# The first sequence's norm, queries and keys of a last attention given out inside the dense layer ahead of it, and maxima that run 30 steps ahead instead of 36

## The chip, the core and the metric

The kernel runs on one core of a Trainium2 chip, in one launch. A core has a matrix engine (TensorE, PE in the profile; its weight loads are counted apart as PEld), three engines for elementwise work (VectorE, DVE; ScalarE, ACT, with the activation functions; GpSimd, POOL), and SyncE (SP), which here issues nearly all transfers. Every engine runs its own list of instructions in order and waits on semaphores for what the others make. The metric is the device time of a launch in microseconds (us); the time of a kernel is the median of its runs.

## The reference

Four sequences of 1024 tokens with 128 features go through two blocks, eight residual layers in all: gated linear attention, mixture of experts, causal softmax attention, the same mixture of experts, then a rotary linear attention, a dense layer, a softmax attention with a linear distance bias ("the last attention"), and the dense layer once more. Ahead of each stands a layer norm without weights. The two layers around the change:

```python
# last attention, on x = _layernorm(x): 16 heads of 8 features
q, k, v = jnp.split(x @ W_attn + b_attn, 3, axis=-1)      # each (4, 1024, 16, 8)
att = jnp.einsum('bqhd,bkhd->bhqk', q, k) * (1.0 / math.sqrt(D))
att = att / temperature
bias = slopes[:, None, None] * rel[None, :, :]            # rel = key position - query position
bias = jnp.where(causal[None, :, :], bias, -jnp.inf)
w = jax.nn.softmax(att + bias[None, :, :, :], axis=-1)
y = jnp.einsum('bhqk,bkhd->bqhd', w, v).reshape(Bc, Tc, Cc)
return y @ W_proj + b_proj
...
# dense layer, on x = _layernorm(x): 128 -> 512 -> 512 -> 512 -> 128, weights of -1, 0, 1 with scales
h = silu(_tlin(x, w1_w, w1_s)) * _tlin(x, w2_w, w2_s)
h = gelu(_tlin(h, h1_w, h1_s)); h = gelu(_tlin(h, h2_w, h2_s))
return _tlin(h, w3_w, w3_s)
```

The causal attention has the same form with 16 heads of 8 query and key features, 64 value features and no bias.

## The kernel before, in words

**Stages.** The activations `k.x` stay on the core throughout. The stages run one behind another, each with its own pools; what of the next layer can be done early is mixed into the layer ahead by hand. A scheduler then orders the instructions of each engine, so that the order in the code is a priority, not the final order.

**Two softmax attentions, one loop.** `softmax_attention` serves the causal ("ca") and the last ("aa") attention. Two heads make a pair; 4 sequences have 32 pairs, and a round of the main loop takes two of them. A round has 24 steps: 12 tiles of (half of the queries, block of 128 keys) for each of its two pairs. A step makes a tile of scores on PE (`product`, L721, and the mask through `hide`, L727), then its exponential on ACT (L849); the products with the values follow (L968 in ca, L1138 in aa).

**Maxima ahead.** The exponential needs each query's largest score. The generator `maxima` computes it apart, with the scores the other way round: 12 steps for a pair (`BY_QUERY`), in each two matmuls (L721, out to `bank`) and two reductions on DVE (L749 with the causal mask, L754 without). When a pair's 12 steps are done, `finish` transposes the result (L763), splits it into a high and a low part (L765 on ACT, L767 on DVE) and writes them with four transfers (L771, SP) into two rows of the pair's query operand; the scores multiply these rows along, and so subtract the maximum. `all_maxima` strings the pairs together; `finish` of a pair comes behind the first step of the next. Ahead of the first round, 36 steps are called (three pairs); after that one step goes with each step of the main loop, until all are used up.

**Operands.** `Pairs` holds six query and six key tiles in turn (`held`). A `prologue(b)` makes a sequence's queries and keys: layer norm (`k.normed`, L104 to L125), transposes (L90), projections (L1100, evacuated with bias on DVE in L1103 and L1105), a split into high and low part (L1106 on ACT, L1107 on POOL), and `lay_out`, eight transfers in all to two images in DRAM, where heads lie in rows (L701). `load(n)` reads a pair's operands back in four transfers (L710). The last attention's prologue also computes the values (L1115, L1119) into a tile that `clear` sets up on POOL (L1089, L1090). Sequence 0's prologue and the loads of four pairs come ahead of the maxima, sequence b+1's in round 4b + 1. Ahead of all of it `alibi_attention` computes the scale from the temperature (L1078, L1079) and multiplies two biases (L1082, L1083).

**The dense layer.** `dense_layer` branches on a flag in memory; the side that runs here takes each product in two parts, high and low. `dense_parts` works in eight lots of 512 tokens with five stages each; 22 ticks with two lanes run two lots side by side, a lane two ticks behind the other. Its lines: input transposes L1383, splits L1390 to L1394, products L1400, the gate L1421 and L1423, the Gelus L1440 to L1446, the output L1453, its transposes L1457 and the residual sum L1460. In the first dense layer a generator `ahead` runs beside: 16 pieces ahead of the ticks, then one with every lane of every tick. It holds the rotary attention, `Rotary.pieces`, 10 pieces for each sequence. Its tables and weights lie in a pool `ra_w` that `third.close()` gives back behind the layer.

Of the kernel before, what the change touches and what calls it, by code (L numbers as in the profile page):

```python
# [25 lines left out]
DK = P // H  # L26
# [9 lines left out]
class Core:  # L36
# [3 lines left out]
    def __init__(self, ctx: ExitStack, tc: tile.TileContext):  # L40
        self.tc, self.nc = tc, tc.nc
        nc = tc.nc
        self.const = ctx.enter_context(tc.tile_pool(name="const", bufs=1))
        self.x = self.const.tile([P, NT, P], F32, name="x")
        self.ident = self.const.tile([P, P], F32, name="ident")
        make_identity(nc, self.ident)
        self.ones = self.const.tile([P, P], F32, name="ones")
        nc.gpsimd.memset(self.ones, 1.0)
        self.turn = 0
        self.mark = []  # L50
# [730 lines left out]
BY_QUERY = [(i, c) for i in range(NB) for c in range(i // 4 + 1)]  # L781
# [1 line left out]


def softmax_attention(
    k: Core, pairs: Pairs, work, ps_e, scale, maxima, prologue, consume, hold, beside, before=lambda b: None
):

    nc = k.nc
    per = H // 2
    count = B * per

    def all_maxima():
        finish = None
# [12 lines left out]
    def some(n=1):  # L812
        for _ in range(min(n, len(later))):
            later.popleft()()

    turn = 0

    prologue(0)
    for n in range(4):
        pairs.load(n)  # L820
    for _ in range(len(BY_QUERY) * 3):
        next(ahead, None)
    late = None
    for first in range(0, count, 2):
        if first % per == 0 and first // per + 1 < B:
            before(first // per + 1)
        if first % per == 2 and first // per + 1 < B:
            prologue(first // per + 1)
        for n in (first + 4, first + 5):
            if n < count:  # L830
                pairs.load(n)
        for c, j in BY_KEY:
            start = max(j * P, c * 512)
            w = (c + 1) * 512 - start
            es = []
# [215 lines left out]
class AlibiWeights:  # L1051
    def __init__(self, k: Core, pool, wq_d, wk_d, wv_d, bq_d, bk_d, bv_d, wo_d, bo_d, temp_d):
        self.wq = k.load(pool, "aa_wq", wq_d)
        self.wk = k.load(pool, "aa_wk", wk_d)
        self.wv = k.load(pool, "aa_wv", wv_d)
        self.bq = k.load(pool, "aa_bq", bq_d)
        self.bk = k.load(pool, "aa_bk", bk_d)
        self.bv = k.load(pool, "aa_bv", bv_d)
        self.wo = k.load(pool, "aa_wo", wo_d)
        self.bo = k.load(pool, "aa_bo", bo_d)  # L1060
        self.scale = k.load(pool, "aa_scale", temp_d.partition_broadcast(P))


def alibi_attention(k: Core, pairs: Pairs, weights: AlibiWeights):

    nc, tc = k.nc, k.tc
    space = bass.MemoryType.PSUM
    with (
# [4 lines left out]
        tc.tile_pool(name="aa_pse", bufs=2, space=space) as ps_e,  # L1073
        tc.tile_pool(name="aa_pso", bufs=1, space=space) as ps_o,
    ):
        wq, wk, wv, wo = weights.wq, weights.wk, weights.wv, weights.wo
        bq, bk, bv, bo, scale = weights.bq, weights.bk, weights.bv, weights.bo, weights.scale
        nc.vector.reciprocal(scale, scale)  # L1078
        nc.vector.tensor_scalar_mul(scale, scale, 1.0 / math.sqrt(DK))  # L1079

        ps = k.bank()
        nc.tensor.matmul(ps[:1, :P], lhsT=bv, rhs=wo, start=True, stop=True)  # L1082
# [7 lines left out]
            nc.gpsimd.memset(v[:, :, :, DK : DK + 1], 1.0)  # L1090

        def prologue(b):
            xnT = k.normed(two, b, 1)
            for which, (w, bias) in enumerate(((wq, bq), (wk, bk))):
                hi = two.tile([P, T], F32R, tag="hi", name="hi", bufs=1)
                lo = two.tile([P, T], F32R, tag="lo", name="lo", bufs=1)
                for c in range(2):
                    cut = slice(c * 512, (c + 1) * 512)
                    ps = k.bank()
                    nc.tensor.matmul(ps, lhsT=w, rhs=xnT[:, cut], start=True, stop=True)  # L1100
                    val = two.tile([P, 512], F32, tag="val", name="val")
                    if which == 0:
                        nc.vector.tensor_scalar(val, ps, bias, scale, ALU.add, ALU.mult)  # L1103
                    else:
                        nc.vector.tensor_scalar(val, ps, bias, None, ALU.add)  # L1105
                    nc.scalar.copy(hi[:, cut], val)  # L1106
                    nc.gpsimd.tensor_sub(lo[:, cut], val, hi[:, cut].bitcast(F32))  # L1107
                pairs.lay_out(b, which, hi, lo)
            v = vs[b % 2]
            if b < 2:  # L1110
                clear(v)
            for t in range(0, NB, 4):
                ps = k.bank()
                for i in range(4):
                    nc.tensor.matmul(  # L1115
                        ps[:, i * P : (i + 1) * P], lhsT=xnT[:, (t + i) * P : (t + i + 1) * P], rhs=wv,
                        start=True, stop=True,
                    )
                nc.scalar.copy(  # L1119
                    v[:, t : t + 4, :, :DK], ps.rearrange("p (t h d) -> p t h d", t=4, d=DK)  # L1120
                )

        held = {}

        def consume(b, r, c, j, es):
# [55 lines left out]

        softmax_attention(
            k, pairs, work, ps_e, 1.0, partial(pairs.maxima, pool=two, steps=BY_QUERY), prologue, consume,
            False, deque(),
        )


# [154 lines left out]
        }  # L1342


def dense_layer(k: Core, f: Dense, name, before=None, out_d=None):

    flag = k.nc.values_load(f.inexact[0:1, 0:1], min_val=0, max_val=1)
    with k.tc.If(flag == 0) as whole:  # L1350
        dense_parts(k, f, name, True, before, out_d)
    with whole.Else():
        dense_parts(k, f, name, False, before, out_d)


def dense_parts(k: Core, f: Dense, name, exact, before, out_d):

    nc, tc = k.nc, k.tc
    nc_h = NH // P
# [3 lines left out]
    with tc.tile_pool(name=f"ff_{name}{n_parts}", bufs=2) as pool, tc.tile_pool(name=f"ff_{name}{n_parts}w", bufs=1) as wp:  # L1363
        w = f.short if exact else f.load(k, wp)
# [105 lines left out]
        def all_before():  # L1470
            for b in range(B):
                yield from before(pool, b)

        ahead = all_before() if before else iter(())
        for _ in range(16):
# [3 lines left out]
        for tick in range(5 * B + 2):  # L1479
            for lane in range(2):  # L1480
                n, stage = divmod(tick - 2 * lane, 5)
                if 0 <= n < B:
                    next(lots[2 * n + lane])
                next(ahead, None)


@with_exitstack
def kernel(ctx: ExitStack, tc: tile.TileContext, a: dict, out: bass.AP):
    k = Core(ctx, tc)
    dram = ctx.enter_context(tc.tile_pool(name="dram", bufs=1, space=bass.MemoryType.DRAM))  # L1490
    wp = ctx.enter_context(tc.tile_pool(name="moe_w", bufs=1))
    if True:
# [46 lines left out]
        pairs = Pairs(k, rows, images, "aa", 6, NEAR)  # L1539
        aa = []  # L1540
        ff_w = ctx.enter_context(tc.tile_pool(name="ff_w", bufs=1, side="right"))
        third = ExitStack()
        ra_w = third.enter_context(tc.tile_pool(name="ra_w", bufs=1, side="right"))
        rotary = []

        def next_layers():
# [18 lines left out]
            rotary[0].bring = bring  # L1565
        moe.close()
        with k.psum("third", 4, 2):
            dense_layer(k, f, "0", rotary[0].pieces)
        third.close()
        alibi_attention(k, pairs, aa[0])  # L1570
        with k.psum("fourth", 4, 2):
            dense_layer(k, f, "1", None, out)


_DENSE = ["ff_w1", "ff_w2", "ff_h1", "ff_h2", "ff_w3"]
# [132 lines left out]
```

## Time and profile before

| | us |
|---|---|
| three runs | 2610.53, 2607.05, 2591.27; median 2607.05 |
| profiled execution | 2596.9 |
| its span, from first to last instruction | 2595.2 |
| PE busy | 2277.0 (88% of the span) |
| PE weight loads | 1252.7 (48%) |
| DVE busy | 1654.5 (64%) |
| ACT busy | 1244.3 (48%) |
| POOL busy | 916.9 (35%) |
| causal attention, first to last exponential's round | 360.8 to 1299.8 |
| first dense layer, its last transposes | 1666.5 |
| last attention, first exponential | 1735.5 |
| last attention, end of the last round | 2371.8 |
| mean granted PE clock | 0.914 |

The profiled execution is one run of its own, so its length differs from the three timed ones. "Busy" is time in which an engine had an instruction running; matmuls are pipelined, so that a busy PE isn't PE at its peak. Times inside the program are counted from the start of the span. A tile is named by what writes it and what it reads: `bank<-aa_k,aa_q` is a matmul of the maxima in the last attention, `scores<-aa_q,aa_k` one of its scores.

### The profile page before, as it was taken

Reading aid. Unit: us, or ns where it says so; the run is one execution under the profiler, and the core shown is the slowest. Engines: PE = TensorE matmul, PEld = TensorE weight load, DVE = VectorE, ACT = ScalarE, POOL = GpSimd, SP = SyncE. Lnnn points to the kernel's source line nnn. Section 1 sums busy time; section 2 is a strip of 40 time slices with the busy share of each in tenths; the row PEclk is TensorE's granted clock in tenths of the full one; section 3 lists DMA queues with packets and bytes.
Section 4 is the critical chain, followed back from the end, with each engine's and each line's share of the span. In section 5 each row is a group of like instructions: output and inputs, shape, how many; then the busy total and the mean of one; then the engine's idle time right before and its main releaser. Section 6 shows DMA issues by size and latency. Waiting matters only on the chain.

```text
span 2595.2 us, 40054 instructions
## 1 busy us (share of the span) xinstructions
PE 2277.0 (88%) x14195; PEld 1252.7 (48%) x14195; DVE 1654.5 (64%) x4765; ACT 1244.3 (48%) x2023; POOL 916.9 (35%) x718
## 2 busy tenths in 40 slices
PE   6885679998899889988967999769999999998988
PEld 4564533443444344343353666535445454544666
DVE  6977266667667757774146665567767767673544
ACT  6552214545445535454422566405545555455865
POOL 2213306787487567768733332300000000000222
PEclk8977859999899989999988999858989999998999
DMA  9300322001201110000050000042103131010000
GB/s 251 108 9 29 102 73 74 26 18 42 73 25 37 58 50 18 18 22 22 1 167 9 9 25 1 5 126 86 46 23 109 32 98 47 23 23 1 9 9 18
DMA packets 92390, 124.81 MB, mean 48 GB/s; under 512 B 13210, under 2 KB 66460, under 8 KB 92172
## 3 DMA queue, kind: packets, MB, share of 16 engines
q1 hardware_dynamic: 88860, 115.76, 15.8%
q0 software_dynamic: 2560, 5.30, 0.6%
q8 instruction: 120, 1.97, 0.3%
q10 hardware_dynamic: 752, 0.98, 0.1%
q14 instruction: 98, 0.80, 0.1%
HBM read 67.57 MB, written 52.85 MB: 46 GB/s over the span
## 4 chain that ended last, share of the span: by engine, by line
PE 54%; DVE 19%; issue 10%; POOL 8%; ACT 5%; DMA 4%; SPq 0%; DVEq 0%; POOLq 0%; ACTq 0%
PE bank L721 9%; PE o L1138 8%; PE o L968 7%; PE scores L721 7%; PE bank L1400 6%; POOL e_first L986 4%; DVE nm L754 3%; DVE junk L749 3%; PE scores L727 2%; PE bank L932 2%; DVE s L250 2%; PE bank L917 1%; POOL slots L505 1%; PE bank L90 1%; DMA back<-answer,given 1%
## 5 line engine op out<-in xcount | busy, mean ns | idle before, releaser
L849 ACT ACTIVATE e<-scores 128x1024 f32<-128x1024 f32 (+3 forms) x704 | 544.5, 791 | 604.6 <-PE scores L727 370.4
L986 POOL TENSOR_TENSOR e_first<-e_first,e 128x1024 f32<-128x1024 f32 (+3 forms) x320 | 542.2, 1723 | 317.2 <-ACT e L849 178.0
L749 DVE CUSTOM_DVE_ANT_0 junk<-bank,mask 128x128 f32<-128x128 f32 (+3 forms) x1024 | 495.4, 484 | 226.8 <-PE bank L721 162.8
L754 DVE TENSOR_REDUCE nm<-bank 128x1 f32<-128x512 f32 x512 | 332.0, 685 | 126.4 <-PE bank L721 117.1
L968 PE MATMUL o<-e,v 128*32 128x512 f32 (+3 forms) x2560 | 299.9, 494 | 0.0
L721 PE MATMUL bank<-aa_k,aa_q 62*128 62x512 f32 (+3 forms) x768 | 238.8, 434 | 44.1 <-DVE nm L754 25.3
L1138 PE MATMUL o<-e,v 128*32 128x512 f32 (+3 forms) x1536 | 227.5, 517 | 0.0
L721 PE MATMUL bank<-ca_k,ca_q 62*128 62x512 f32 (+3 forms) x768 | 195.5, 422 | 31.2 <-DMA ca_k<-ca_k 14.0
L721 PE MATMUL scores<-ca_q,ca_k 64*128 64x512 f32 (+3 forms) x768 | 182.2, 444 | 36.1 <-ACT e L849 32.3
L721 PEld LDWEIGHTS scores<-ca_q,ca_k 64*128 64x128 f32 x768 | 78.3, 188 | 260.2 <-ACT e L849 185.3
L727 PE MATMUL scores<-halves 64*128 64x128 f32 x2048 | 199.8, 260 | 0.0
L727 PEld LDWEIGHTS scores<-halves 64*128 64x128 f32 x2048 | 193.1, 194 | 10.1 <-issue 0.3
L1107 POOL TENSOR_TENSOR lo<-val,hi 128x512 fp32r<-128x512 f32 x16 | 20.1, 1274 | 442.1 <-ACT hi L1106 260.1
L721 PEld LDWEIGHTS bank<-aa_k,aa_q 62*128 62x128 f32 x768 | 121.4, 203 | 109.0 <-DVE nm L754 53.0
L721 PE MATMUL scores<-aa_q,aa_k 64*128 64x512 f32 (+3 forms) x768 | 164.9, 415 | 2.2 <-ACT e L849 2.0
L1446 DVE TENSOR_TENSOR h<-val,h 128x512 fp32r<-128x512 f32 x128 | 90.9, 717 | 107.8 <-ACT h L1445 78.0
L1006 DVE RECIPROCAL raw<-raw 128x128 f32<-128x128 f32 x128 | 117.5, 937 | 55.1 <-ACT raw L1002 42.7
L1400 PE MATMUL bank<-h,ff_h1s 128*128 128x512 f32 x512 | 135.4, 408 | 15.4 <-POOL h L1394 10.4
L1390 POOL CAST h<-gate 128x512 fp32r<-128x512 f32 x32 | 27.5, 861 | 335.5 <-DVE gate L1423 326.9
L721 PEld LDWEIGHTS scores<-aa_q,aa_k 64*128 64x128 f32 x768 | 80.1, 193 | 135.4 <-issue 67.5
L721 PEld LDWEIGHTS bank<-ca_k,ca_q 62*128 62x128 f32 x768 | 97.5, 201 | 89.8 <-DVE nm L749 36.5
L1440 ACT ACTIVATE val<-bank,ff_t 128x512 f32<-128x512 f32 x128 | 88.1, 689 | 93.3 <-PE bank L1400 84.6
(276 smaller groups left out, 3724.6 us busy)
## 6 DMA issues: line engine op xcount, KB each, us to landing
aa_q<-aa_q SPq DMA_DIRECT2D x64, 208.0 KB
ca_q<-ca_q SPq DMA_DIRECT2D x64, 128.0 KB
ca_k<-ca_k SPq DMA_DIRECT2D x64, 128.0 KB
aa_k<-aa_k SPq DMA_DIRECT2D x64, 128.0 KB
wi<-in_moe_wi_dram SPq DMA_DIRECT2D x16, 256.0 KB
wo<-in_moe_wo_dram SPq DMA_DIRECT2D x16, 256.0 KB
back<-blank SPq DMA_DIRECT2D x8, 512.0 KB
got<-back SPq DMA_DIRECT2D x8, 512.0 KB
```

The costliest lines, as they stand in the source:

```text
L721: self.k.nc.tensor.matmul(out, lhsT=lhsT, rhs=rhs, start=True, stop=stop, skip_group_check=True)
L727: self.k.nc.tensor.matmul(ps, lhsT=part[:, 0, :], rhs=part[:, 1, :], start=False, stop=(a == 1), skip_group_check=True,)
L749: nc.vector.tensor_tensor_reduce(junk[:, :cols], ps[:, :cols], self.mask[:, 512 - cols :], -1.0, 3e38, ALU.add, ALU.min, to,)
L754: nc.vector.tensor_reduce(to, ps[:, :cols], AX.X, ALU.max, negate=True)
L849: power = nc.scalar.activation(e[:, :, :w], ps[:, :, :w], AF.Exp, scale=scale)
L968: nc.tensor.matmul(outs[which][32 * i : 32 * i + 32, skip:], lhsT=v[:, j, i, 32 * which : 32 * which + 32], rhs=es[i // 2][:, i % 2, : 512 ...
L986: nc.gpsimd.tensor_add(to, to, es[i][:, :, : 512 - skip])
L1006: nc.vector.reciprocal(part, part)
L1138: nc.tensor.matmul(o[32 * i : 32 * i + 32, skip:], lhsT=v[:, j, 4 * r + i, :], rhs=es[i // 2][:, i % 2, : 512 - skip], start=(j == 0), sto ...
L1400: nc.tensor.matmul(ps, lhsT=weights[:, c, :], rhs=inputs[c][i], start=(s == 0), stop=(s == len(steps) - 1))
L1440: nc.scalar.activation(val, ps, AF.Gelu, scale=s[:, o : o + 1])
L1446: nc.vector.tensor_sub(nxt[1][:, o, :], val, hi.bitcast(F32))
```

## The change

Five edits:

- The body of the last attention's prologue becomes a generator `alibi_front`, without the values; it norms in two halves of four blocks. Sequences 1 to 3 call it from `prologue` in one go, and `values` behind it.
- For sequence 0 it is run as `alibi_ahead`, which `dense_layer` takes as `then` and appends to the pieces beside the first dense layer, behind the rotary's 40. It has five pieces (the norm, the transposes, the queries, the keys, the loads of four pairs), in ticks 12 to 14 of 0 to 21. Whatever is left is run behind the ticks.
- There it borrows tiles: `Other` maps the tags `xn`, `hi`, `lo` and `val` to the rotary's `ra_xn`, `ra_qT`, `ra_v` and `ra_other`, one buffer each, and the transposed input goes into the rotary's cosine table. `ra_w` therefore stays open to the end of the kernel.
- `softmax_attention` gets `begun`: the last attention no longer calls `prologue(0)` and the first loads.
- Ahead of the first round, both attentions call 30 steps of maxima instead of 36.

```diff
 def softmax_attention(
-    k: Core, pairs: Pairs, work, ps_e, scale, maxima, prologue, consume, hold, beside, before=lambda b: None
+    k: Core, pairs: Pairs, work, ps_e, scale, maxima, prologue, consume, hold, beside, before=lambda b: None,
+    begun=False,
 ):
...
-    prologue(0)
-    for n in range(4):
-        pairs.load(n)
-    for _ in range(len(BY_QUERY) * 3):
+    if not begun:
+        prologue(0)
+        for n in range(4):
+            pairs.load(n)
+
+    for _ in range(len(BY_QUERY) * 2 + 6):
         next(ahead, None)
...
+def alibi_front(k: Core, pairs: Pairs, weights: AlibiWeights, pool, b, to=None):
+    nc = k.nc
+    xn = pool.tile([P, NB, P], F32, tag="xn", name="xn", bufs=1)
+    for i in range(0, NB, 4):
+        k.layernorm(pool, xn[:, i : i + 4, :], k.x[:, b * NB + i : b * NB + i + 4, :], 4)
+    yield
+    weights.xnT = xnT = to or pool.tile([P, T], F32, tag="xnT", name="xnT", bufs=1)
+    k.transpose(xnT, [xn[:, t, :] for t in range(NB)])
+    yield
+    for which, (w, bias) in enumerate(((weights.wq, weights.bq), (weights.wk, weights.bk))):
+        hi = pool.tile([P, T], F32R, tag="hi", name="hi", bufs=1)
+        lo = pool.tile([P, T], F32R, tag="lo", name="lo", bufs=1)
+        for c in range(2):
...
+            val = pool.tile([P, 512], F32, tag="val", name="val", bufs=2)
...
+        pairs.lay_out(b, which, hi, lo)
+        yield
+
+def alibi_ahead(k: Core, pairs: Pairs, weights: AlibiWeights, pool, table):
+    tags = {
+        "xn": ("ra_xn", 1), "hi": ("ra_qT", 1), "lo": ("ra_v", 1), "val": ("ra_other", 1),
+    }
+    pool = Other(pool, tags)
+    weights.invert(k)
+    yield from alibi_front(k, pairs, weights, pool, 0, table)
+    for n in range(4):
+        pairs.load(n)
...
         def prologue(b):
-            xnT = k.normed(two, b, 1)
...
+            for _ in alibi_front(k, pairs, weights, two, b):
+                pass
+            values(b, weights.xnT)
+
+        def values(b, xnT):
             v = vs[b % 2]
...
+        values(0, weights.xnT)
...
-            False, deque(),
+            False, deque(), begun=True,
...
         def all_before():
             for b in range(B):
                 yield from before(pool, b)
+            if then:
+                yield from then(pool)
...
+        for _ in ahead:
+            pass
...
-        third = ExitStack()
-        ra_w = third.enter_context(tc.tile_pool(name="ra_w", bufs=1, side="right"))
+        ra_w = ctx.enter_context(tc.tile_pool(name="ra_w", bufs=1, side="right"))
...
-            dense_layer(k, f, "0", rotary[0].pieces)
-        third.close()
+            dense_layer(
+                k, f, "0", rotary[0].pieces, lambda pool: alibi_ahead(k, pairs, aa[0], pool, rotary[0].cosT)
+            )
```

More of the change, by code (lines that the diff above doesn't have):

```diff
@@ L1060, in __init__, with invert, tile @@
         self.bo = k.load(pool, "aa_bo", bo_d)
-        self.scale = k.load(pool, "aa_scale", temp_d.partition_broadcast(P))
+        self.temp = k.load(pool, "aa_temp", temp_d.partition_broadcast(P))
+        self.scale = pool.tile([P, 1], F32, name="aa_scale")
+    def invert(self, k: Core):
+        k.nc.vector.reciprocal(self.scale, self.temp)
+        k.nc.vector.tensor_scalar_mul(self.scale, self.scale, 1.0 / math.sqrt(DK))
+class Other:
+    def __init__(self, pool, tags):
+        self.pool, self.tags = pool, tags
+    def tile(self, shape, dtype, tag, name, bufs=None):
+        tag, number = self.tags.get(tag, (tag, bufs))
+        return self.pool.tile(shape, dtype, tag=tag, name=name, bufs=number)
@@ new lines, in alibi_front @@
+def alibi_front(k: Core, pairs: Pairs, weights: AlibiWeights, pool, b, to=None):
[11 more added lines that the diff above has]
+        for c in range(2):
+            cut = slice(c * 512, (c + 1) * 512)
+            ps = k.bank()
+            nc.tensor.matmul(ps, lhsT=w, rhs=xnT[:, cut], start=True, stop=True)
+            val = pool.tile([P, 512], F32, tag="val", name="val", bufs=2)
+            if which == 0:
+                nc.vector.tensor_scalar(val, ps, bias, weights.scale, ALU.add, ALU.mult)
+            else:
+                nc.vector.tensor_scalar(val, ps, bias, None, ALU.add)
+            nc.scalar.copy(hi[:, cut], val)
+            nc.gpsimd.tensor_sub(lo[:, cut], val, hi[:, cut].bitcast(F32))
+        pairs.lay_out(b, which, hi, lo)
+        yield
@@ L1075, in alibi_attention @@
     ):
[L1076 to L1079, printed above, removed]
+        wv, wo, bv, bo = weights.wv, weights.wo, weights.bv, weights.bo
         ps = k.bank()
@@ L1092, in prologue @@
         def prologue(b):
-            xnT = k.normed(two, b, 1)
[L1094 to L1108, printed above, removed]
+            for _ in alibi_front(k, pairs, weights, two, b):
+                pass
+            values(b, weights.xnT)
+        def values(b, xnT):
             v = vs[b % 2]
@@ L1342, in load, with dense_layer, dense_parts @@
         }
-def dense_layer(k: Core, f: Dense, name, before=None, out_d=None):
+def dense_layer(k: Core, f: Dense, name, before=None, then=None, out_d=None):
     flag = k.nc.values_load(f.inexact[0:1, 0:1], min_val=0, max_val=1)
     with k.tc.If(flag == 0) as whole:
-        dense_parts(k, f, name, True, before, out_d)
+        dense_parts(k, f, name, True, before, then, out_d)
     with whole.Else():
-        dense_parts(k, f, name, False, before, out_d)
-def dense_parts(k: Core, f: Dense, name, exact, before, out_d):
+        dense_parts(k, f, name, False, before, then, out_d)
+def dense_parts(k: Core, f: Dense, name, exact, before, then, out_d):
     nc, tc = k.nc, k.tc
@@ L1567 @@
         with k.psum("third", 4, 2):
-            dense_layer(k, f, "0", rotary[0].pieces)
-        third.close()
+            dense_layer(
+                k, f, "0", rotary[0].pieces, lambda pool: alibi_ahead(k, pairs, aa[0], pool, rotary[0].cosT)
+            )
         alibi_attention(k, pairs, aa[0])
         with k.psum("fourth", 4, 2):
-            dense_layer(k, f, "1", None, out)
+            dense_layer(k, f, "1", out_d=out)
 _DENSE = ["ff_w1", "ff_w2", "ff_h1", "ff_h2", "ff_w3"]
```

## The prediction

> **What bounds the kernel now.** I read the page's slices first. TensorE (PE) works 88% of the span; its dip in the 26th and 27th of 40 slices (64.9 us each, so 1622 to 1752; 7 and 6 tenths) lies where the first dense layer hands over to the last attention, and the granted clock dips with it (8 and 5):
>
> ```profile
> PE   6885679998899889988967999769999999998988
> PEclk8977859999899989999988999858989999998999
> ```
>
> Then the chain of waits from 1590 to 1900 us (start, length, what). The dense layer's last matmuls (L1457) end at 1666.8; norm, queries, keys and a run of transfers follow, rows to memory and back as operands, until the first matmul of the maxima (L721):
>
> ```profile
> 1666.91 2.83 issue
> 1670.60 1.48 issue
> 1678.28 2.29 PE bank L90 x8
> ...
> 1687.42 6.03 DMA aa_q<-lo
> 1693.61 2.49 POOL lo L1107 x2
> 1696.67 5.50 DMA aa_k<-lo
> 1702.25 2.24 DMA aa_k<-aa_k
> 1704.62 3.24 PE bank L721 x7
> ```
>
> So 1704.6 - 1666.8 = 37.8 us pass, most of it on DMA and POOL. Third, the windows: busy time of PE, PE's weight loads, VectorE (DVE), ScalarE (ACT), POOL, then clock.
>
> ```profile
> 1680.00:1690.00 10.00, 6.73 (x27) 3.88 (x25) 9.94 (x36) 2.76 (x6) 2.55 (x2) 0.84 0.42 136
> 1690.00:1700.00 10.00, 0.00 (x0) 0.00 (x0) 2.87 (x22) 1.34 (x3) 2.48 (x2) 0.50 0.83 256
> 1710.00:1720.00 10.00, 8.47 (x17) 4.46 (x16) 8.59 (x26) 0.00 (x0) 0.00 (x0) 0.50 0.32 80
> 1760.00:1770.00 10.00, 10.00 (x47) 5.10 (x46) 5.15 (x17) 2.39 (x6) 0.00 (x0) 0.50 0.00 0
> ```
>
> DVE is full from 1680 to 1690: it takes the norm statistics of all four sequences in the gap (32 of L104 start from 1670.3 to 1691.3), not just the first. After the gap, maxima run at half clock with PE and DVE both near 85%, and full clock returns at 1770. Last, how quickly a row of maxima is ready (transpose L763, then its last row write on SP):
>
> ```profile
> 1855.33 0.28 PE L763 MATMUL bank<-ident,least 128*16 128x128 f32 x1
> 1858.35 0.62 SPq L771 DMA_DIRECT2D aa_q<-nm_lo  x1
> ```
>
> **The change, part by part.** Times are against the profiled execution, 2596.9 us (span 2595.2 and 1.7 around it); the three runs' median, 2607.05, lies 10.2 above it.
>
> *The front leaves the gap.* In the built program the first sequence's projections, eight row writes and the reads of four pairs stand well ahead of the dense layer's branch end. The layer has 22 ticks with two pieces each; of the 40 rotary pieces 16 go ahead of them, so the rotary ends in the 12th tick and the front takes the next three. The lot that ends in the 15th tick has its last transposes (L1457) at 1606.3, the layer's last at 1666.5: 60 us lie behind the front, and transfers of 6.0, 5.5 and 2.2 us end there unseen. On SP they pass only rotary's four fetches, issued before. PE needs after the branch only the bias product and the eight value matmuls (0.27 each, L1115, at most twice that at half clock): ready for maxima by 1670.4 + 4 = 1674.5.
>
> But DVE is not. In the built order 16 L104 (0.26), 8 L105 (0.16), two chains of small operations (L107, L110, L113 to L116, some 0.85 each), the bias sum (0.24) and one L125 (0.34) stand ahead of the first maximum. From 1672.1 (the exit and a 1.5 us issue gap stay) that is 4.2 + 1.3 + 1.7 + 0.6 = 7.8, so about 1679.5. The first L749 was at 1705.1: **-25.6**.
>
> *Norms of the other sequences lose their cover.* Behind that, among the maxima, stand another 7 L125 (2.4), 8 L105 (1.3), 8 L104 (2.1) and two chains (2.0): 7.8 us in a stretch where DVE has some 15% free. Between 0 (the half-clock PE hides them) and 7.8, I take half: **+4**. ACT gets two Sqrt in mid-attention, with four table loads of 1.28 (none there before); at 0 to 2 us busy of 10 there I put them at +1, bound 0 to 5.1.
>
> *30 steps for 36, last attention.* Twelve steps are a pair's: L763 of the first two pairs lie at 1720.6 and 1735.8, 15.2 us, so 1.27 a step. Six fewer: **-7.5**. They run at the end instead: the two-pair rounds, by the starts of their exponentials (L849), take 35.7 us with 24 steps of maxima, 30.6 with 12, 26.8 with none, so 0.4 a step, **+2.4**.
>
> *The same, causal attention.* L763 at 347.3 and 361.5 give 1.18 a step, **-7**. At the end, rounds 14 and 15 take 55.2 and 52.1 although with 12 and no steps; full rounds take 48.5 to 49.1. In round 14 PE waits 2.35 us for POOL's L1012, behind a queue of L986. Six steps of PE work put in just there cost between +3 (at 0.5 each) and -5 (the round falls toward 49): I take **-1**.
>
> *The dense layer grows.* PE: 8 transposes (1.09 at 1793.2) and four projections (1.98 + 1.88): 5. ACT: 0.6 + 4 x 0.62 + 2 x 0.21 + two to four table loads of 1.28 = 6 to 9. DVE: 8 x (0.26 + 0.16 + 0.34) + two chains + 0.7 + 4 x 0.75 = 11.5. POOL: 4 x 1.25 = 5. PE is 92% busy there (18.09 and 18.76 of 20 us from 1620), so its 5 count nearly in full; the rest is half hidden, but the stand-in tiles have one buffer: a second `val` waits for POOL's subtraction on DVE, with the dense layer's h splits queued behind it, and key `hi` waits on ACT for the query writes' landing (6.0) with Gelus behind. From +5 to +14; **+8**, near the PE price.
>
> Extra layer norm calls in halves, `invert` moved and the rotary weights kept to the end cost nothing: the first lies in the DVE rows counted, the others change no waiting instruction.
>
> Sum: -25.6 + 4 + 1 - 7.5 + 2.4 - 7 - 1 + 8 = **-25.7**, about -26, so 2571 on the profiled execution and 2581 on the median of the runs. I predict between: **2576**. What is late next is DVE, then the half clock, which both stay.
>
> [...] The row: from 1710 to 1770 PE was 85 to 100% busy and was granted 0.50 throughout but for some 4 us near 1745; full clock came at 1681.8, after 3.5 us without a gap, and at 1770, again after four. [...]
>
> **Rivals.**
>
> *Full clock early.* With operands ready, values and maxima stream without a gap and the clock returns some 30 us sooner. PE is the limit at half clock from 1738 to 1770 (windows 8.9 to 10 of 10), worth 15 us: 2561. For it: 1681.8. Against: DVE-paced maxima have gaps. [...]
>
> *Cover gone.* All 7.8 of the norms on the path, tables 5, dense +14, causal tail +3: -25.6 + 7.8 + 5 - 7.5 + 2.4 - 7 + 3 + 14 = -8, 2589 to 2599, so 2594. For it: DVE is in order, and the maxima behind it pace PE. Against: PE at half clock has the same load.
>
> *Not ready in time (slower).* Row writes of a pair are needed by the scores at the next round's start. Thirty steps leave five steps between, not eleven. By rows of the steady round, the fifth-last product (1864.5) lies 7.7 us before that score (1872.2). L763 to the end of the last issue is 1858.97 - 1855.33 = 3.6, with landing (nearest row 2.24) 5.9. If SP holds the eight operand reads of the next pairs (1869.41 to 1872.70, 3.3 us) ahead of them and POOL or ACT adds 0.9, PE waits 10.1 - 7.7 = 2.4 us a round. Over 30 rounds that is +72: 2576 + 72 = 2648. It decides from 0.9 us a round, where it eats the 26. For it besides: nine of the 64 pairs took 10.1 to 16.0 us from transpose to last issue, SP standing behind a prologue's or the MoE's transfers. Against: that is once a sequence, not each round, and in the built SP order the row writes stand ahead of the reads.
>
> *It does not do what it says.* Reads that must be waited for at the branch end would bring back up to 14 us. The built order leaves those 60 us; I fold it into the second rival.
>
> **How the numbers follow.** Forecast 0.45, full clock early (with it a better causal tail) 0.16, cover gone 0.28, not ready in time 0.11. The range takes the first three and the bounds of the costs: dense from +5 to +14, tails from -5 to +3, and the runs' own 19 us spread: **2552 to 2604**. A measurement of this kernel tells about 1% from no change, 26 us, just where the forecast lies; so it is split, 0.27 faster and 0.18 same. Faster: 0.27 + 0.16 + 0.03 of cover gone = 0.46. Same: 0.18 + 0.25 = 0.43. Slower: 0.11.
>
> **What the changed profile would show.** First L749 of the last attention some 13 us behind the last L1457 (38 before); 17 or 18 maxima steps before the first exponential; clock 0.5 until the second round; the dense layer 5 to 14 us longer; the first causal round near 60 us (67.2 before) and round 14 near 50; no PE wait for a DMA at round starts. Wrong: a first L749 later than 20 us behind the branch, L763 more than 7 us from its landing, or a dense layer that grows by more than 14.

## The result and the profile after

The changed kernel takes 2578.6 us in the median of 15 runs (2565.0 to 2602.62), the kernel before 2607.05 us (15 runs, 2591.27 to 2612.11). The ratio is 0.9917, 95% interval 0.9897 to 0.9937. By the ratio the change is worth 22 us; the two medians lie 28 apart. The forecast was 2576, range 2552 to 2604. Two far slower executions, of 3275.7 us in run e10 and of 8371.04 us in run e11 below, are left out of all ratios.

The profiled executions alone would say something else: 2596.9 us before and 2599.55 after. The one lies 10 us under the median of its kernel, the other 21 us above. A second profiled execution of the changed kernel (run e8 below) took 2564.39. The first view is therefore the span and the mean granted clock of the changed kernel's profile, then the same of its second profile:

```profile
core 0: 2597.8 us, clock 0.911
```

```profile
core 0: 2562.7 us, clock 0.925
```

Same program, 35 us apart, and the clock differs. Added up from the clock's records, PE stood at 0.50 for 463 us in the first and for 389 us in the second (448 in the kernel before). So a stage is compared below together with its time at half clock, and sums are taken from timed runs.

In the changed kernel's file some lines have other numbers: L849 is L852 there, and L1457, the dense layer's last transposes, is L1506. The page's slices of the changed kernel:

```profile
PE   6775679999999889999967999899999999998998
PEclk8987869999889989988988999968989889898999
```

The 26th and 27th slices, 7 and 6 tenths before, hold 8 and 9 (64.9 us each); the clock in the 27th is still low, 6. The chain of waits at the hand-over (start, length, what):

```profile
1675.99 0.68 PE bank L1506 x4
1676.76 2.96 issue
1680.18 0.49 DVE ln_stats L104 x2
1681.70 0.43 DVE ln_ve L107
1682.35 1.28 ACT L109
1685.48 0.31 DVE xn L125
1686.06 3.20 PE bank L721 x5
```

The transfers aa_q<-lo and aa_k<-lo and POOL's L1107 are gone from the chain. Behind the dense layer's last transposes (L1506) stand the branch exit, then the norm of the next sequence on DVE, with ACT's table load in it, then the maxima. The first maximum on DVE, before and after, comes 38.6 and 9.3 us behind the start of the last of those transposes (1666.53 and 1676.38):

```profile
1705.10 0.29 DVE L749 CUSTOM_DVE_ANT_0 junk<-bank,mask 128x128 f32<-128x128 f32 x1 [11.78 <-PE bank L721]
```

```profile
1685.71 0.28 DVE L749 CUSTOM_DVE_ANT_0 junk<-bank,mask 128x128 f32<-128x128 f32 x1
```

What is late next is DVE, as predicted. The windows behind it (PE, weight loads, DVE, ACT, POOL, then clock):

```profile
1690.00:1700.00 10.00, 8.51 (x17) 4.55 (x17) 8.98 (x31) 0.00 (x0) 0.00 (x0) 0.50 0.00 0
1710.00:1720.00 10.00, 9.59 (x22) 3.54 (x20) 6.75 (x27) 1.28 (x2) 0.00 (x0) 0.50 0.01 2
```

By the records PE is busy for 85 and 96% of these two stretches and DVE for 90 and 68%, and the clock stays at half, as before. And the rows of maxima, transpose and last write, in a steady round:

```profile
1844.11 0.28 PE L763 MATMUL bank<-ident,least 128*16 128x128 f32 x1
1847.54 0.62 SPq L771 DMA_DIRECT2D aa_q<-nm_lo  x1
```

That is 4.05 us, 3.65 before. But the second exponential of a round, the first that needs the row of the round's second pair, now follows that row's transpose by 9.0 us in the steady rounds of the last attention (18.0 before), and by 12.6 in the causal one (24.1 before).

Stages by the starts of their instructions, in us, in brackets the time at half clock in them ("front" is the early front, "ca" and "aa" 30 steps in the causal and in the last attention; profile 1 and 2 are the changed kernel):

| stage | before | ca alone | ca + aa | front | front + ca | profile 1 | profile 2 |
|---|---|---|---|---|---|---|---|
| causal rounds 0, 1 | 130.1 (17) | 132.4 (10) | 135.1 (17) | 136.1 (28) | 138.1 (20) | 138.0 (20) | 135.0 (17) |
| causal rounds 2 to 13 | 701.6 (85) | 693.1 (79) | 700.5 (99) | 700.5 (92) | 700.8 (102) | 700.7 (99) | 686.9 (58) |
| causal rounds 14, 15 | 107.3 (3) | 102.4 (0) | 102.3 (0) | 107.3 (3) | 102.5 (0) | 102.3 (0) | 102.5 (0) |
| to the first dense product | 116.6 (44) | 112.4 (34) | 115.6 (41) | 120.9 (48) | 118.9 (41) | 119.0 (41) | 119.1 (44) |
| dense layer to its last transposes | 250.1 (3) | 252.1 (14) | 250.7 (3) | 256.0 (7) | 255.7 (7) | 254.8 (0) | 255.7 (7) |
| to the first maximum (L749) | 38.6 (30) | 37.7 (29) | 37.7 (27) | 9.3 (7) | 9.3 (7) | 9.3 (7) | 9.3 (7) |
| first maximum to round 2 | 131.7 (62) | 132.6 (66) | 122.2 (47) | 135.1 (65) | 137.5 (68) | 130.5 (68) | 130.5 (61) |
| last attention, rounds 2 to 13 | 477.6 (41) | 478.4 (41) | 483.9 (41) | 476.6 (38) | 474.1 (31) | 499.2 (82) | 477.8 (24) |
| rounds 14, 15 | 57.4 (0) | 58.9 (3) | 61.3 (3) | 58.9 (3) | 59.0 (3) | 60.0 (0) | 61.3 (3) |

### The profile page after: what moved, and what is told of

The parts are those of the page before. It is cut to its first block, busy times and chain, and to the rows that moved or that the text cites. A ratio compares the mean times of both kernels' runs of the same rounds, so it can differ in the third digit from the quotient of the medians.

```text
span 2597.8 us, 40051 instructions
## 1 busy us (share of the span) xinstructions
PE 2308.3 (89%) x14195; PEld 1258.5 (48%) x14195; DVE 1659.5 (64%) x4789; ACT 1254.4 (48%) x2033; POOL 918.6 (35%) x718
## 5 line engine op out<-in xcount | busy, mean ns | idle before, releaser
L852 ACT ACTIVATE e<-scores 128x1024 f32<-128x1024 f32 (+3 forms) x704 | 545.7, 792 | 619.1 <-PE scores L727 316.0
L749 DVE CUSTOM_DVE_ANT_0 junk<-bank,mask 128x128 f32<-128x128 f32 (+3 forms) x1024 | 497.1, 485 | 211.4 <-PE bank L721 142.9
L971 PE MATMUL o<-e,v 128*32 128x512 f32 (+3 forms) x2560 | 304.8, 496 | 0.0
L721 PE MATMUL bank<-aa_k,aa_q 62*128 62x512 f32 (+3 forms) x768 | 248.1, 442 | 21.5 <-DVE nm L754 13.6
L1186 PE MATMUL o<-e,v 128*32 128x512 f32 (+3 forms) x1536 | 228.1, 537 | 0.0
L721 PE MATMUL scores<-aa_q,aa_k 64*128 64x512 f32 (+3 forms) x768 | 177.3, 434 | 5.5 <-ACT e L852 5.4
L1107 POOL TENSOR_TENSOR lo<-val,hi 128x512 fp32r<-128x512 f32 x16 | 20.2, 1277 | 431.4 <-ACT hi L1106 404.9
L721 PEld LDWEIGHTS bank<-aa_k,aa_q 62*128 62x128 f32 x768 | 122.0, 208 | 103.4 <-DVE nm L754 57.1
## 6 DMA issues: line engine op xcount, KB each, us to landing
wi<-in_moe_wi_dram SPq DMA_DIRECT2D x16, 256.0 KB
wo<-in_moe_wo_dram SPq DMA_DIRECT2D x16, 256.0 KB
```

The lines of the kernel that those rows point to most:

```text
L721: self.k.nc.tensor.matmul(out, lhsT=lhsT, rhs=rhs, start=True, stop=stop, skip_group_check=True)
L749: nc.vector.tensor_tensor_reduce(junk[:, :cols], ps[:, :cols], self.mask[:, 512 - cols :], -1.0, 3e38, ALU.add, ALU.min, to,)
L971: nc.tensor.matmul(outs[which][32 * i : 32 * i + 32, skip:], lhsT=v[:, j, i, 32 * which : 32 * which + 32], rhs=es[i // 2][:, i % 2, : 512 ...
L1186: nc.tensor.matmul(o[32 * i : 32 * i + 32, skip:], lhsT=v[:, j, 4 * r + i, :], rhs=es[i // 2][:, i % 2, : 512 - skip], start=(j == 0), sto ...
```

## The experiments

All are timed in five rounds against the kernel before on the same chip. The ratios are those of the runs to the runs before, with their 95% intervals.

**The parts alone and in pairs.** The number of steps is one line:

```diff
-    for _ in range(len(BY_QUERY) * 2 + 6):
+    for _ in range(len(BY_QUERY) * 3):                      # e1: 36 in both
+    for _ in range(len(BY_QUERY) * (3 if begun else 2) + (0 if begun else 6)):   # e3: 36 in the last
+    for _ in range(len(BY_QUERY) * (2 if begun else 3) + (6 if begun else 0)):   # e5: 36 in the causal
```

e2 and e6 edit the same line in the kernel before (30 in both, 30 in the causal one); e8 is the changed kernel unedited.

Expected of e1:

> The changed kernel with 36 steps ahead in both attentions: the early front alone. Prediction's account: the front is worth 25.6 less 13 of added costs (12.6 us) and the 30 steps the other 13, so about 2594. Theory from the two profiles: the first exponential of the causal attention did not come earlier with 30 steps (348.8 after, 348.0 before), so the steps in it are worth nothing, and those in the last attention some 5; the front carries the rest: about 2584 (ratio 0.991 to 0.992). Rival: the steps are worth less than nothing, since later rounds lose their lead; then this kernel is faster than the changed one, 2570 to 2575.

Expected of e2:

> The kernel before with 30 steps ahead in both attentions and no early front. Prediction's account: -7.5 + 2.4 in the last attention and -7 - 1 in the causal one, so 2594 (ratio 0.995). Theory from the profiles: nothing in the causal attention, -5 in the last: 2602 (0.998). Rival, the lead is too short: 2612 or more.

Expected of e3:

> The changed kernel with 36 steps ahead in the last attention, 30 in the causal one. Against the front alone it prices the 30 steps of the causal attention: prediction -8, theory 0. Against the changed kernel it prices those of the last one: prediction +5, theory +5, rival -5 or less.

Expected of e5:

> The early front, with 30 steps in the last attention and 36 in the causal one. If the two numbers of steps act on their own stage alone: the front alone (0.992) plus what the last attention's 30 steps cost behind it, 0 (prediction: -5) to +10 us (changed kernel against 30 in the causal one alone: 0.9917 against 0.988). So 2589 by the prediction, 2595 to 2600 if 30 steps hurt behind the front. In the trace: rounds 2 to 13 of the last attention some 15 to 20 us longer than the 475 of the kernels with 36, with more half-clock time, if the loss is a steady one; 477 + 4 if the long profile of the changed kernel was chance.

Expected of e6:

> The kernel before with 30 steps in the causal attention alone. If those carry what both together gained without the front (0.9943): 0.994 to 0.996, with the last two causal rounds at 102.3 us (107.3 before), first rounds unchanged. If the last attention carried it: 0.998 to 1.0.

Expected of e8:

> The changed kernel once more, on the same chip as the others. Ratio 0.990 to 0.994. Rounds 2 to 13 of the last attention: 499 us again, with some 80 us at half clock, if 30 steps behind the front bring that about; 478 to 485 if it was chance of one execution.

| run | front | causal | last | ratio | interval |
|---|---|---|---|---|---|
| e1 | early | 36 | 36 | 0.9922 | 0.9891 to 0.9953 |
| e6 | late | 30 | 36 | 0.9952 | 0.9930 to 0.9974 |
| e2 | late | 30 | 30 | 0.9943 | 0.9920 to 0.9965 |
| e3 | early | 30 | 36 | 0.9880 | 0.9847 to 0.9913 |
| e5 | early | 36 | 30 | 0.9961 | 0.9934 to 0.9988 |
| e8 | early | 30 | 30 | 0.9892 | 0.9849 to 0.9934 |

The front is worth about 0.8% alone (20 us). The causal attention's 30 steps are worth 0.4 to 0.7% in each of three pairs (before to e6, e1 to e3, e5 to the changed kernel at 0.9917 or 0.9892). The last attention's 30 steps show no gain in any pair outside the intervals: 0.1% better (e6 to e2), 0.4% worse (e1 to e5), 0.1 to 0.4% worse (e3 to the two measurements of the changed kernel). The theory put down ahead of e1, that the causal steps are worth nothing, falls: it had looked at the head of the stage alone. The fear behind e5, that 30 steps bring 15 to 20 us of half clock into rounds 2 to 13, falls with e8: 477.8 us with 24 us at half clock, against 499.2 with 82 in the first profile. That was chance of one execution. (e8's ratio, 0.9892, lies a little outside the 0.990 to 0.994 expected of it, its interval does not.)

**The norms of the other sequences (e4).** They wait for the last exponential of the round before their prologue:

```diff
-            nc.vector.bn_stats(stats[:, t, :], src[:, t, :])
+            self.behind(nc.vector.bn_stats(stats[:, t, :], src[:, t, :]), behind)   # alibi_front: k.mark if b else ()
```

> The changed kernel in which the norm statistics of sequences 1 to 3 wait for the exponential of the round before their prologue, so that they no longer stand among the first maxima. If they cost 4 us or more there (DVE in order, prediction +4, its second rival 7.8): 2571 to 2575, and the first exponential of the last attention comes 4 to 8 us sooner behind the first L749. If PE at half clock hides them: 2579, first exponential unmoved. If they cost as much where they land now, among the rounds: 2579 with an earlier first exponential.

Ratio 0.9933 (0.9909 to 0.9957). The first L749 came 3.9 us behind the dense layer's last transposes instead of 9.3. But the first exponential came 34.5 us behind them instead of 35.7, and round 2 137.2 us instead of 139.8 (61 us at half clock, 75 and 68 in the two profiles of the changed kernel). So of the 5.4 us that these norms take ahead of the first maximum, 1.2 reached the first exponential and 2.6 round 2: PE at half clock hides a good part of them. And rounds 5 and 9, where the norms now stand, took 50.9 us each (35.8 and 39.6 in the second profile), rounds 4 and 8 42.1 and 43.3 (49.8 and 49.5): 7 us lost in the one pair of rounds and 5 in the other, each with 7 us more at half clock. The norms found no better cover among the rounds.

**PE kept busy at the hand-over (e7).** On top of e3, three matmuls whose result nobody reads stand at the end of the dense layer's branch:

```diff
         for _ in ahead:
             pass
+        if then:
+            ps = k.bank()
+            for _ in range(3):
+                nc.tensor.matmul(ps, lhsT=k.ident, rhs=k.x[:, -4:, :].rearrange("p t d -> p (t d)"), start=True, stop=True)
```

> Early front, 30 steps in the causal attention, 36 in the last, and three matmuls behind the dense layer's last sum, inside its branch, whose result nobody reads, so that PE stands still for under 2 us at the branch end instead of 3.2 (some 3 us of added PE work). Rival 'full clock early': granted clock 1.0 in the first 20 us behind the branch, and 10 to 15 us less up to the third round, ratio 0.983. Theory: the clock is halved by the maxima's own gaps (DVE paces them), so that it falls to 0.5 within 10 us of the branch whatever comes ahead: ratio 0.988 to 0.990.

Ratio 0.9911 (0.9880 to 0.9943), no better than e3. The windows of this kernel around the hand-over, in the columns used above:

```profile
1650.00:1660.00 10.00, 8.16 (x30) 5.04 (x29) 3.13 (x5) 2.87 (x5) 3.91 (x4) 1.00 0.02 6
1660.00:1667.00 7.00, 3.59 (x23) 2.27 (x21) 6.00 (x42) 2.54 (x5) 3.09 (x3) 1.00 0.02 5
1667.00:1677.00 10.00, 7.17 (x13) 3.61 (x13) 9.75 (x53) 0.41 (x2) 0.00 (x0) 0.51 0.00 0
```

The standstill at the branch's end is down to 0.78 us (2.9 to 3.5 in the other runs), but PE runs dry right behind it:

```profile
1661.71 2.05 PE L1162 MATMUL bank<-aa_wv,ra_cosT 128*128 128x128 f32 x16
1665.68 0.49 PE L721 MATMUL bank<-aa_k,aa_q 62*128 62x128 f32 x3 [1.92 <-DVE aa_bo L1141]
1669.19 3.12 PE L721 MATMUL bank<-aa_k,aa_q 62*128 62x256 f32 x5 [3.03 <-DVE nm L749]
```

Behind the value products PE waits 1.92 us for DVE, works for 0.49 and waits 3.03 us for DVE again; the clock falls at 1667.3, in the middle of that. First maximum to round 2 took 144.8 us, 90 of them at half clock. So e7 did not keep PE busy over the hand-over, and by itself it does not decide the rival. The second profile of the changed kernel (e8) does more: there the clock was granted in full at 1667.6, as the first maxima ran, and was gone 3.4 us later; the same happened once more from 1701.7 on. The two windows, and the longest wait of PE in them:

```profile
1667.56:1670.97 3.41, 2.08 (x6) 1.03 (x6) 3.41 (x23) 0.48 (x1) 0.00 (x0) 1.00 0.00 0
1701.69:1705.10 3.41, 2.63 (x8) 1.00 (x7) 2.53 (x13) 0.25 (x1) 0.00 (x0) 1.00 0.01 2
```

```profile
1669.19 0.91 PE L721 MATMUL bank<-aa_k,aa_q 62*128 62x256 f32 x2 [0.71 <-DVE nm L749]
```

In the first, DVE was busy throughout, with the rest of the norm and the first maxima, and PE for 2.08 of 3.41 us; PE stood still for at most 0.71 us at a time, and the next 30.7 us ran at half clock. In the second, among the maxima, PE was busy for 2.63 us, and the next 23.9 us ran at half clock. So in this execution full clock did come early, and was lost at the pace that DVE sets for PE. That speaks against the rival; a hand-over in which PE never runs dry was not run.

**SP's queue ahead of the branch (e9, e12).** The table above has a row that the prediction did not have: from the last causal exponential to the first dense product it is 118.9 to 122.0 us in the eight profiles that have the early front and nothing done about what follows, and 112.4 to 116.6 in the three without the front. SP's own queue in the changed kernel shows why:

```profile
1357.32 0.36 SPq L139 DMA_DIRECT2D aa_wq<-in_aa_wq_dram  x1
...
1361.52 0.33 SPq L139 DMA_DIRECT2D aa_temp<-in_aa_temp_dram  x1
1362.44 0.38 SPq L563 DMA_DIRECT2D got<-back  x1
```

and in the kernel before:

```profile
1351.33 0.82 SPq L1554 DMA_DIRECT2D aa_k<-krows_r  x2
1358.29 0.40 SPq L563 DMA_DIRECT2D got<-back  x1
```

The last attention's weights and key rows (nine of L139, ten of twelve of L1606) are now read inside the dense layer's branch, so they must be issued ahead of it; before, the scheduler had put them near 1505 us. The rotary attention's first read (got) stands behind them. From the issue of the experts' last scatter (L615) to the issue of that read it is 4.6 to 5.0 us in the three without the front and 9.3 to 10.8 in the eight, and to the first sum that uses the read (L570) 9.0 to 9.4 against 14.0 to 15.4. The stretch as a whole grew by less from before to profile 1 and 2, 2.4 and 2.5 us, because the last scatter came sooner there (50.2 and 52.1 us behind the last exponential, with 5 and 11 us at half clock, against 53.9 with 17). e9 gives these loads to ACT's queue; e12 leaves them on SP and issues them inside the branch, behind that read:

```diff
-        self.wq = k.load(pool, "aa_wq", wq_d)
+        self.wq = k.load(pool, "aa_wq", wq_d, k.nc.scalar)      # e9: so all nine, and the key rows
...
+        def beside(pool, b):                                    # e12
+            if b == 2:
+                for t in pairs.k_:
+                    for g in range(2):
+                        k.nc.sync.dma_start(t.bitcast(F32)[64 * g : 64 * g + NEAR, :], krows_r.bitcast(F32))
+                aa[0].fetch(k)                                  # the nine weights
+            yield from rotary[0].pieces(pool, b)
```

Expected of e9:

> Early front, 30 steps in the causal attention, 36 in the last, and the last attention's weight and key-row loads (nine of L139, twelve of L1606) issued by ACT instead of SP. In the kernel before SP issued them near 1505 us, inside the dense layer; with the early front they stand ahead of the branch, and SP issues 19 of them (1353.6 to 1361.9) ahead of the first read of the rotary attention (got). Theory: that queue is why the stretch from the last causal exponential to the first dense product grew from 112 to 117 us to 119 to 122; so 114 to 117 here, ratio 0.986 (0.988 with them on SP). Rival: the branch itself takes longer, since it holds more code: 119 to 121 again, ratio 0.988.

Expected of e12:

> Early front, 30 steps in the causal attention, 36 in the last, and the last attention's weight and key-row loads issued by SP inside the dense layer's branch, right behind the first read of the rotary attention, so that neither SP ahead of that read nor ACT among the Gelus pays for them. Theory (the queue on SP): from the last scatter of the experts (L615) to the rotary's first sum (L570) some 9 us (8.7 before, 13.5 with the change, 9.9 with ACT), from the last causal exponential to the first dense product 113 to 117 us, ratio 0.985 to 0.988. Rival: the time lies elsewhere; 119 us again, ratio 0.988 to 0.991.

e9: from scatter to read 5.5 us, but the last scatter came 54.4 us behind the last causal exponential (50.2 to 53.3 in the eight), and the stretch stayed at 118.5; ratio 0.9912 (0.9878 to 0.9946). ACT issued the loads among the Gelus of the experts; whether that held the scatter up is open, since e11 below, with the same loads on ACT, has it at 51.3 and the stretch at 115.8. e12: 4.7 us from scatter to read, 9.5 to the sum, and 113.8 for the stretch; ratio 0.9870 (0.9828 to 0.9911). Its SP queue:

```profile
1350.09 0.38 SPq L563 DMA_DIRECT2D got<-back  x1
1350.61 5.89 SPq L1629 DMA_DIRECT2D aa_k<-krows_r  x12
```

The queue on SP is shown as the cause of the 5 us between scatter and sum: they come with the loads ahead of the read in all eight and go in e12. The whole stretch says less, since e12's has 34 us at half clock and those of the eight 41 to 48; and in the whole time e12 cannot be told from e3 (0.9880).

**How short a lead can be (e10, e11).** 26 steps in both (`* 2 + 2`), and e9 with 42 in the last:

Expected of e10:

> The changed kernel with 26 steps ahead in both attentions, the least with which the first round's rows are asked for ahead of it; a pair's rows are then asked for in the last step of the round before. If rows that come too late make a wait (prediction's rival 'not ready in time'): PE waits at round starts for a transfer, 3 to 8 us a round, steady causal rounds of 52 or more (49.0 with 30), steady rounds of the last attention of 39 or more (36.0), and 2620 to 2700 in all. If not, the causal tail falls once more (102.5 to 98) and the last attention's steady rounds move by less than 1 us: ratio 0.987 to 0.992.

Expected of e11:

> As the one with the loads on ACT, but 42 steps ahead in the last attention. If each six steps there cost 6 us at the head and give back 6 in the steady rounds and 2 to 3 in the tail (30 against 36): 0 to -4 against it. If the gain from 30 to 36 was the place of single steps in a round and not the lead: steady rounds within 35.4 to 36.0, head +6, so +4 to +6.

e10: ratio 1.0561 (1.0520 to 1.0601), 2747.3 us. Steady causal rounds take 59.7 to 61.7 us (49.0), those of the last attention 38.7 (36.0). Lines of its timeline at the start of causal round 3, from the transpose of the odd pair's maxima on:

```profile
548.84 0.28 PE L763 MATMUL bank<-ident,least 128*16 128x128 f32 x1
...
552.82 0.62 SPq L771 DMA_DIRECT2D ca_q<-nm_lo  x1
...
557.19 0.49 PE L721 MATMUL scores<-ca_q,ca_k 64*128 64x512 f32 x1
...
559.64 1.02 ACT L852 ACTIVATE e_first<-scores 128x1024 f32<-128x1024 f32 x1 [4.40 <-PE scores L727]
```

The last write of the row is issued by 553.4, and the scores start 3.7 us later, 8.35 us behind the transpose; ACT has stood for 4.4. In this round the second exponential comes 8.7 us behind the first, with 30 steps (profile 2) 1.9. The trace holds no landing for these writes, and other matmuls stand ahead of these scores in PE's list, so how much of the 3.7 us is landing and how much the place that the scheduler gave the scores isn't shown; a wait of PE for a transfer at the round's start, as expected, is not among its waits. Transpose to second exponential is 10.8 us; with 30 steps it was 12.6. So a lead that is too short costs time, as the rival "not ready in time" has it, and that begins between 26 and 30 steps; how much 30 steps have to spare isn't shown, since in the last attention the 9.0 us at 30 steps are even fewer than e10's 10.1.

e11: ratio 0.9934 (0.9912 to 0.9955), against e9's 0.9912: a little slower or the same. Steady rounds 36.0, as with 30 steps, rounds 0 and 1 125.1 (64 at half clock) against 111.7 (52), rounds 14 and 15 57.2 against 58.6. So the 0.3 us of a steady round (35.7 with 36) do not come from a short lead; that they come from where single steps fall in a round is likely, not shown.

## Why the prediction was right, and where not

The time and the range held: the sum of 26 us was 22 (5 either way). But its terms were partly others than those predicted, and part of the agreement is luck: a gain of 7 us that isn't there and costs of 6 and 5 us that were left out were made up for by a front, a causal tail and a dense layer that each came out 2 to 4 us better, and by 5 us that no term explains.

- *The front leaves the gap, -25.6.* Right, and more: 38.6 to 9.3 us, **-29.3** (9.3 in every kernel with the front but e4 and e7, which change the hand-over). The first norm statistics came 3.8 us behind the transposes instead of the 5.6 forecast, and from them to the first maximum it took 5.5 us (1680.2 to 1685.7) instead of 7.8; the bias and value products were hidden beside it. (The prediction's own 1672.1 + 7.8 is 1679.9, so its terms give -25.2.)
- *Norms and tables, +4 and +1, and 30 steps in the last attention, -7.5.* At about the same half clock (61 to 68 us), first maximum to round 2 takes 131.7 and 132.6 without the front, 135.1 and 137.5 with front and 36 steps, 130.5 twice in the changed kernel: +3 to +5 and -5 to -7. Right in size by these rows; e4, which takes the norms away from there, gained only 2.6 us up to round 2.
- *Last attention's tail, +2.4.* Right: 57.4 to 59.0 with 36, 60.0 to 61.3 with 30. The term that is missing is the middle: at equal half clock rounds 2 to 13 take some 6 us more with 30 steps (483.9 against 478 at 41 us; 480.5 in e5 against 474.1 at 31), 36.0 against 35.7 in the steady rounds and 39.6 against 35.3 in round 9. So the 30 steps of the last attention gave back what they took, where the prediction had -5.
- *Causal attention, -7 at the head.* This step failed. "L763 at 347.3 and 361.5 give 1.18 a step" is a right rate for steps that nobody waits for: the first exponential comes behind 25 steps of maxima whether 36 or 30 are called ahead (360.8 and 361.6 us), and the other 35 or 29 run inside round 0, which takes 67.1 to 68.0 us either way, with 36 steps 17 or 18 us of them at half clock, with 30 steps 7 or 8; what sets that length isn't shown. In the last attention the same 25 stand ahead (22.5 with the front, where the prediction's signs had 17 or 18), but there round 0 is paced by the maxima, and the gain is real.
- *Causal tail, -1 with a bound of -5.* At its bound: 107.3 to 102.3 us; round 14 falls from 55.2 to 48.5, round 15 rises from 52.1 to 53.8. In round 14 PE's wait of 2.4 us for L1012 is gone, and PE is busy for 46.7 us there (second profile) instead of 52.6, with 386 matmuls for 382, and without the 3 us at half clock:

```profile
1192.50:1247.70 55.20, 52.63 (x382) 21.86 (x384) 21.32 (x55) 24.71 (x37) 41.10 (x27) 0.97 0.01 2
1182.20:1230.90 48.70, 46.70 (x386) 19.94 (x388) 28.21 (x73) 24.79 (x36) 38.20 (x25) 1.00 0.01 2
```

- *The dense layer, +8.* +4.7 to +6.0, the price of PE's matmuls alone, which was the lower bound; ACT, DVE and POOL were hidden, and the single buffers cost nothing that shows.
- *"On SP they pass only rotary's four fetches."* This step failed: the front also pulled 19 loads ahead of the branch, +5 us between scatter and sum, shown by e12.
- *Full clock early, 0.16.* It did not come: 61 and 68 us at half clock up to round 2 in the two profiles, and profile 2 lost the full clock that it had. In the profile before, too, the full clock at 1770 stands behind more than the four us that the prediction gives: PE had no gap from 1752.9 on, 17.1 us, all at half clock. *Cover gone, 0.28.* Of its costs only the norms' came, 3 to 5 us by the rows above, the rest not. *Not ready in time.* Not at 30 steps, where the steady rounds take 49.0 and 36.0 us (48.5 to 49.1 and 35.7 before); at 26 it costs 5.6%. The prediction had 5.9 us from transpose to landing; in e10 the scores start 8.35 us behind the transpose, the landing itself isn't in the trace.

The shown terms make -29.3 - 1.2 (131.7 to 130.5) + 6 + 2.6 - 5 + 5 + 5 = -17 us. The rest of the 22 isn't placed: timed runs of the kernel before have a mean clock of 0.912, those of the changed kernel of 0.919, and 0.01 goes with some 16 us from run to run; whether the higher clock is a cause or goes with the shorter gaps isn't shown. Of the 0.4 to 0.7% that 30 causal steps bring, the tail's 5 us (0.2%) is shown; whether the remainder is less half clock in rounds 2 to 13 (85 to 96 us with 36 steps, 58 to 102 with 30) stays open. At about the same half clock these rounds are 3 to 7 us shorter with 30 steps (700.5 at 99 against 703.4 at 96 in e5; 694.3 at 82 in e9 against 701.6 at 85), but rounds 0 and 1 are 5 us longer (135.1 against 130.1, both at 17).

## What to carry to other kernels

A rate between two events is a gain only if the stage waits for the second: look first how many steps really stand ahead of the first consumer in the built order. The work that was moved into a branch here pulled the loads it reads ahead of that branch, so walk the queue at the branch's entry and not only at its end; issuing those loads inside, behind the first urgent one, gave the 5 us back. A lead can be near its edge without a line in the profile that says so: from making a row to its first exponential it was 24.1 us with 36 steps in the causal attention, 12.6 with 30 and 10.8 with 26, and only the last of these made the steady rounds longer, by some 11 us. And see that an experiment did what it was made for: e7 took one standstill of PE away, and its trace shows two others right behind.

## What was not expected of the hardware

The granted clock differs between executions of the same program: 389 and 463 us at half clock in two profiles, and not in the same places (24 and 82 us in rounds 2 to 13 of the last attention, 58 and 99 in those of the causal one). Over 127 executions of eleven sets of runs, 0.01 of mean clock goes with 16.2 us within a kernel (correlation -0.86), and most of a kernel's own spread, 18 to 38 us, goes with it. Nor does one length of standstill go with a fall of the clock. In the second profile it fell behind 3.41 us in which PE was busy for 2.08 and stood still for at most 0.71 at a time. In e7 it fell at 1667.3, in a standstill of 3.03 us; ahead of that PE had worked for 0.49 and stood still for 1.92. What decides when it falls isn't shown.
